# An interaction-layer kernel on one core: where a block's x is loaded, when two table copies are issued, and in which order TensorE prepares the weights

## The chip, the core and the metric

The kernel runs on one core of a Trainium2 chip. The metric is the device time of one execution in microseconds; it is 734.55 us before the change (median of 3 runs, 734.49 to 734.55). The engines are named as in the profile: PE is the matrix engine, PEld its weight loads, DVE the vector engine, ACT the scalar engine, POOL the general-purpose engine, SP the engine that only issues transfers. A "q" behind an engine's name is its sequencer, which issues transfers.

## The reference

For 1024 samples with F = 39 fields of E = 64 numbers, three layers each multiply every channel by every field and mix the products. The output is a weighted sum of the channels of all layers:

```
X0 = sparse_embedding                                    # (1024, 39, 64)
Xk = X0
for W, b in ((W0, b0), (W1, b1), (W2, b2)):              # 64 channels each
    Xk = einsum('bhe,bfe,ohf->boe', Xk, X0, W) + b
    outs.append(Xk.sum(axis=-1))
return concatenate(outs) @ fc_w.T + fc_b                 # (1024, 1)
```

Only sums over e and over the last layer's channels are needed, so the last two layers can be contracted with the weights before x is touched. With V2[h,f] = sum over o of fc_w2[o] W2[o,h,f], and T[k,g,f] = sum over h of V2[h,f] W1[h,k,g], the third layer's share is the sum over k of X1[k] times a quadratic form of x with the weights T[k]. The second layer's share is the sum over k of X1[k] times a linear form in x. The kernel therefore computes, for each column (one sample, one e), 128 quadratic forms of x: 64 with W0 and 64 with T. It multiplies the halves with each other and sums over e.

## The kernel before, in words

**Stream.** The 65,536 columns are cut into 32 blocks of 2048. A block's x lies in a DRAM table `xd` as 39 rows of 2048 numbers and a row of ones (40 rows for each block, two blocks in one table, three tables). POOL gathers rows of the table into five tiles of 128 partitions (`roll`, L176; an indirect transfer each, L172). Their row labels are such that products of two tiles (six pairs of tiles, `PAIRS`) hold nearly all products of two fields; the rest comes from two smaller tiles `u` and `v`, once for two blocks (`roll_small`, L181). DVE makes a product `p` of 128 x 2048 (L217), and PE multiplies it with a chunk of the weights `wa` in four quarters of 512 columns (L557), six chunks a block. Four products are in flight (`AHEAD`, the pool `prods`). When a block's six chunks and the small chunk (L577, L588) are done, ACT and DVE finish it (`finish`, L611). PE, DVE, ACT and POOL each run their instructions in the order written.

**Start.** The first block is special. Its x is loaded in two halves, each into a small table `xh` of its own (`load_half`, L248, on ACT's queue, among the loads of `w2s`, `w0s` and `w1s`). POOL gathers tiles 0 to 3 of it half by half from `xh` (L385: gathers 1 to 4 for the first half, 5 to 8 for the second). Between gathers 4 and 5 it issues `load(1, nc.gpsimd)` (L387), the load of the second block's x (1248 rows of 256 bytes, DRAM to DRAM, into `xd`). SP copies both halves from `xh` into the table `xd` as soon as they have landed (L389). Tile 4 of the first block is gathered from that table (`roll(0, (4,))`, L390), then `u` and `v`, which need both blocks' rows, and the five tiles of the second block (`roll(1)`, L470). Behind these POOL loads the biases, and writes the row of ones of the third table (`fill_ones(2, ...)`, L476).

**Weights.** Meanwhile PE and DVE prepare the weights, in this chain: `fc2` from `fc_w` (L353); PE contracts W2 with it into `pv` (L399); DVE transposes that into `blocks` (L420); PE spreads it over the partitions (`spread_v2`, L433); DVE multiplies it with a mask into `v2` (L448); PE multiplies W1 with `v2` (L480), which gives T; DVE transposes T in four pieces into `flat` (L489); ACT and DVE copy these into `both` (L496, L499). W0 goes through seven transposes on PE (`turn_w0`, L411) and four ACT copies into the other half of `both` (L459). Then `weight_rows` (L513) adds symmetric entries into `pairs`, a chunk at a time, `weight_turn` (L534) transposes a chunk on PE, and ACT copies it into `wa`. `spin` (L274) gives PE a matmul of constants whose result nobody reads; a dummy.

**First products.** For the first three chunks the products are made in pieces: two of 512 columns or one of 1024 in the first half, and the second half (1024 columns each, L687) only behind all of these. PE runs the first two quarters of the chunks 0, 1 and 2 (L692), then the other two of each. From chunk 3 on (`steps[3]`, L688) products are whole.

**Waiting.** Transfers issued by POOL count on eight semaphores in turn, so a ninth one waits until the first has landed. POOL's transfers share one queue (q0 in the profile), SP's are on q1, ACT's on q10.

The lines that set what waits for what in the first block's x:

```
for k, cols in enumerate(halves):
    for i in range(4):
        gather_rows(rt[0][:, i, cols], xh[k], i)
    if not k:
        load(1, nc.gpsimd)
for k in (1, 0):
    nc.sync.dma_start(xd[0][0:F, halves[k]], xh[k])
roll(0, (4,))
```

Of the kernel before, what the change touches and what calls it, by code (L numbers as in the profile page):

```python
# [54 lines left out]
F32 = mybir.dt.float32  # L55
I32 = mybir.dt.int32
AF = mybir.ActivationFunctionType
ALU = mybir.AluOpType
AX = mybir.AxisListType

B, F, E, H = 1024, 39, 64, 64
FH = F * H
FT = F + 1
# [3 lines left out]
NT = 5  # L67
# [8 lines left out]
MM = 512  # L76
# [69 lines left out]
def cin_kernel(ctx: ExitStack, tc: tile.TileContext, x, w0t, b0, w1, b1, w2, b2, fc_w, fc_b, out):  # L146
    nc = tc.nc
# [3 lines left out]
    const = ctx.enter_context(tc.tile_pool(name="const", bufs=1))  # L151
# [6 lines left out]
    xd = [dram.tile([2 * FT, BLK], F32, name=f"xd{k}") for k in range(NTAB)]  # L158
    xh = [dram.tile([F, SUB], F32, name=f"xh{k}") for k in range(2)]
# [4 lines left out]
    def load(n, engine=nc.sync):  # L164
        first = n % 2 * FT
        engine.dma_start(  # L166
            xd[n // 2 % NTAB][first : first + F].rearrange("f (b e) -> f b e", e=E),
            xv[:, n * BB : (n + 1) * BB, :],
        )

    def gather_rows(dst, table, k):
        nc.gpsimd.indirect_dma_start(  # L172
            dst, None, table, bass.IndirectOffsetOnAxis(ap=lists[:, k : k + 1], axis=0)
        )

    def roll(n, tiles=range(NT)):  # L176
        for i in tiles:
            k = n % 2 * NT + i
            gather_rows(rt[n % 2][:, i], xd[n // 2 % NTAB][: FT if k < NT else 2 * FT], k)

    def roll_small(n):  # L181
        table = xd[n // 2 % NTAB].rearrange("f (t c) -> (f t) c", c=SUB)
        for k, dst in enumerate((ut, vt)):
            gather_rows(dst[n // 2 % 2], table, 2 * NT + k)
# [6 lines left out]
    bias = const.tile([H, 2], F32, name="bias")  # L191
    b1s = const.tile([128, 1], F32, name="b1s")
    b0s = const.tile([128, 1], F32, name="b0s")
    fc0s = columns[:, 1:2]
    fcb = const.tile([1, 1], F32, name="fcb")
# [3 lines left out]
    lists = const.tile([128, 2 * NT + 2], I32, name="lists")  # L199
# [4 lines left out]
    ones = const.tile([16, 2, 128], F32, name="ones")  # L204
    ones1 = const.tile([16, 2, 128], F32, name="ones1")

    both = const.tile([128, F * FT], F32, name="both")
    pairs = const.tile([128, NCHUNK, 128], F32, name="pairs")
    unit = const.tile([128, 128], F32, name="unit")
# [13 lines left out]
    with prep as prep:  # L223
# [24 lines left out]
        def load_half(k):  # L248
            nc.scalar.dma_start(
                xh[k].rearrange("f (b e) -> b f e", e=E), x[k * SB : (k + 1) * SB]  # L250
            )
# [3 lines left out]
        nc.scalar.dma_start(w0s, w0t.rearrange("b (s a) h -> (b s) (a h)", s=NW))  # L255
        nc.scalar.dma_start(w1s, w1.rearrange("o (s n) -> (o s) n", s=2))
        load_half(1)
        nc.gpsimd.iota(place, pattern=[[0, 1]], base=0, channel_multiplier=1)
        nc.gpsimd.iota(apart, pattern=[[1, 128]], base=0, channel_multiplier=-1)
        nc.scalar.copy(warm, warm)  # L260
# [13 lines left out]
        def spin(n=1, cols=MM // 2):  # L274
            for _ in range(n):
                nc.tensor.matmul(  # L276
                    idle[:, 0:cols],
                    nc.const_aps.tensor(1.0, (128, 128), F32),
                    nc.const_aps.tensor(1.0, (128, cols), F32),
                    start=True,  # L280
                    stop=True,
                )
# [9 lines left out]
        def new():  # L292
            used[0] += 1
            return tmp[:, used[0] - 1 : used[0]]
# [7 lines left out]
        def fused(out, x, scalar, y, op0, op1):  # L302
            nc.vector.scalar_tensor_tensor(out, x, scalar, y, op0, op1)
# [15 lines left out]
        def turn(dst, row):  # L319
            nc.tensor.matmul(dst, row, one, start=True, stop=True)  # L320
# [4 lines left out]
        def turn_twice(at, row, k):  # L325
            turn(small[:, at : at + 1], row[:, k].rearrange("p h s -> p (h s)"))
# [7 lines left out]
        bothv = both.rearrange("p (a b) -> p a b", b=FT)  # L334
        nc.gpsimd.memset(bothv[0:H, :, F], 0.0)
        turn_twice(0, fcrow2, 1)
        spin()

        nc.vector.tensor_copy(row, place)
        step(row, F, 1.0, j)  # L340
# [20 lines left out]
        def fill_ones(k, engine, src):  # L361
            engine.dma_start(xd[k][F::FT].rearrange("r (p c) -> p r c", c=128), src)
# [10 lines left out]
        r, most, seat, far = (new() for _ in range(4))  # L373
        both_of = prep.tile([128, 2], F32, name="both_of")
        jumps = prep.tile([128, 2], F32, name="jumps")
# [6 lines left out]
        halves = [slice(0, SUB), slice(SUB, BLK)]  # L382
        for k, cols in enumerate(halves):
            for i in range(4):
                gather_rows(rt[0][:, i, cols], xh[k], i)  # L385
            if not k:
                load(1, nc.gpsimd)  # L387
        for k in (1, 0):
            nc.sync.dma_start(xd[0][0:F, halves[k]], xh[k])  # L389
        roll(0, (4,))  # L390

        blocks = prep.tile([128, 2, 320], F32, name="blocks")
        w2v = w2s.rearrange("p (h f) -> p h f", f=F)
        for k in range(2):
            for u in range(2):
# [6 lines left out]
                    stop=True,  # L404
                )

        turn_twice(6, fcrow2, 0)

        def turn_w0(k):
            n = min(128, NF * H - k * 128)  # L410
            nc.tensor.transpose(  # L411
                pw[k // 4][0:n, k % 4 * NW * F : (k % 4 + 1) * NW * F],
                w0s[:, k * 128 : k * 128 + n],
                unit[0 : NW * F, 0 : NW * F],
            )

        for k in range(3):
            turn_w0(k)
        for k in range(2):
            nc.vector.transpose(  # L420
                blocks[:, k].rearrange("p (f h) -> p f h", h=32),
# [4 lines left out]
        step(row, 64.0, 2.0 * FT - 1.0, far)  # L426
        nc.vector.tensor_reduce(jumps, steps_at, AX.X, ALU.add)
        fused(most, r, 4.0, most, ALU.add, ALU.add)
        column = blocks.rearrange("h k (f j) -> h (k f) j", j=32)[:, :, 0]

        def spread_v2(u, lo, n):
            rows = slice(H * u, H * u + H)
            nc.tensor.matmul(  # L433
                pv[u][:, 0:n],
                twice[rows].rearrange("p h s -> p (h s)"),
                column[rows, lo : lo + n],
                start=True,
                stop=True,
            )

        spread_v2(0, 0, 20)
        spread_v2(1, 1, 19)
        for k in range(3, 7):
            turn_w0(k)
        spin(1, MM // 4)
        nc.vector.tensor_scalar(v2v[:, 0, :, F - 32], mask, small[:, 6:7], None, ALU.mult)
        for u, at, low, lo, n in ((0, 0, 1, 0, 20), (1, 0, 1, 20, 12), (1, 12, 0, 0, 7)):
            nc.vector.tensor_tensor(  # L448
# [7 lines left out]
        for k, n in enumerate((8, 5)):  # L456
            for t in range(2):
                m = (n + 1 - t) // 2
                nc.scalar.copy(  # L459
                    both3[0:H, :, 8 * k + t : 8 * k + t + 2 * m - 1 : 2, 0:F],  # L460
                    pw[k][H * t : H * t + H, 0 : m * NW * F].rearrange(
                        "h (a b s) -> h s a b", b=F, s=NW
                    ),
                )
        nc.vector.tensor_tensor(seat, seat, far, ALU.add)
        nc.vector.tensor_tensor(both_of[:, 0:1], most, jumps[:, 0:1], ALU.add)
        nc.vector.tensor_tensor(both_of[:, 1:2], both_of[:, 0:1], jumps[:, 1:2], ALU.add)
        nc.vector.tensor_scalar(lists[:, 2 * NT :], both_of, 2.0, seat, ALU.mult, ALU.add)
        roll_small(0)
        roll(1)  # L470
        for h in (0, H):
            nc.gpsimd.dma_start(b0s[h : h + H], b0.rearrange("(h o) -> h o", o=1))
        for k, t in enumerate((b1, b2)):
            nc.gpsimd.dma_start(bias[:, k : k + 1], t.rearrange("(h o) -> h o", o=1))
        nc.gpsimd.dma_start(fcb, fc_b.rearrange("(p o) -> p o", o=1))
        fill_ones(2, nc.gpsimd, ones)  # L476
        w1v = w1s.rearrange("o (h f) -> o h f", f=F)
        groups = [(k, min(NA * k, F - NA)) for k in range(4)]
        for k, a in groups:
# [8 lines left out]
        for k, a in groups:  # L488
            nc.vector.transpose(  # L489
                flat[:, k], pt[k][:, 0 : 32 * NA].rearrange("p (h f) -> p f h", f=NA)  # L490
            )
        for k, a in groups:
            new = NA * k - a
            rows = slice(NA * k, a + NA)
            copy = nc.scalar.copy if k < 3 else nc.vector.tensor_copy
            copy(bothv[H:128, rows, 0:32], flat[H:128, k, new:])  # L496
            if k > 1:
                first = slice(0, 3) if k == 2 else slice(k, k + 1)
                nc.scalar.copy(  # L499
                    bothv[H:128, NA * first.start : rows.stop, 32:FT].rearrange(  # L500
                        "h (k a) b -> h k a b", k=first.stop - first.start
                    ),
                    flat[0:H, first, new:, 0 : FT - 32],
                )
# [164 lines left out]
    p = {}  # L669
# [18 lines left out]
    n, c = steps[3]  # L688
# [8 lines left out]
    for at, (n, c) in enumerate(steps[:-TAIL]):  # L697
# [33 lines left out]
        if at + AHEAD < len(steps):  # L731
            n, c = steps[at + AHEAD]
# [70 lines left out]
```

## Time and profile before

| | us |
|---|---|
| median of the runs (3) | 734.55 |
| the profiled execution's own time | 734.99 |
| its span, from first to last instruction | 733.2 |
| PE busy | 727.5 (99%) |
| DVE busy | 638.9 (87%) |
| POOL busy | 377.6 (51%) |
| ACT busy | 167.7 (23%) |
| mean transfer rate | 269 GB/s |
| one matmul record of L557, 128x512, two for each quarter | 0.594 (0.429 from start to start) |
| product on DVE, 128x2048 | 2.28 |
| product on DVE, 128x1024 | 1.22 |
| gather's issue on POOL, median | 0.94 |

Times inside the span are counted from its first instruction. [...] An idle time in brackets is that of the engine just before the instruction, with what ended it.

### The profile page before, as it was taken

The page shows a single profiled execution, that of the slowest core. Times are in us where ns is not written, and L with a number is a line of the kernel's source. Part 1 is how long each engine was busy: PE and PEld are TensorE (multiplying, and loading weights), DVE is VectorE, ACT ScalarE, POOL GpSimd, SP SyncE. Part 2 cuts the span into 40 slices and gives each one's busy share as a digit, 9 for nine tenths or more (in the row PEclk, how much of TensorE's full clock was granted, in tenths as well). Part 3 has the DMA queues.
Part 4 walks back from the last instruction along what each step waited for, and adds up shares of the span by engine and source line. Part 5 has one row for each costly group of instructions (what it writes and reads, how often), then busy time and mean ns, then how long its engine had stood idle before and what let it go on. Part 6 is the DMA issues. An engine that isn't in the chain of part 4 may idle for free.

```text
span 733.2 us, 6352 instructions
## 1 busy us (share of the span) xinstructions
PE 727.5 (99%) x2377; PEld 314.9 (43%) x2377; DVE 638.9 (87%) x520; ACT 167.7 (23%) x241; POOL 377.6 (51%) x254
## 2 busy tenths in 40 slices
PE   9999999999999999999999999999999999999998
PEld 4344444444444444444444444444444444444443
DVE  6998889988889888898988889888898888889885
ACT  3332121222212222121221212221122221212222
POOL 6858754537555455654547545455654447535300
PEclk9999999999999999999999999999999999999999
DMA  8999967779585796757778676886767876566700
GB/s 264 419 296 381 377 263 276 282 286 323 223 279 238 287 354 261 264 236 265 310 286 299 236 286 228 313 347 224 274 244 276 314 286 259 201 270 245 287 0 1
DMA packets 65979, 197.23 MB, mean 269 GB/s; under 512 B 40109, under 2 KB 40174, under 8 KB 45980
## 3 DMA queue, kind: packets, MB, share of 16 engines
q0 software_dynamic: 28784, 185.56, 65.5%
q1 hardware_dynamic: 35464, 9.28, 5.5%
q10 hardware_dynamic: 1700, 1.99, 0.9%
q8 instruction: 18, 0.29, 0.2%
q14 instruction: 13, 0.11, 0.0%
HBM read 196.76 MB, written 10.60 MB: 283 GB/s over the span
## 4 chain that ended last, share of the span: by engine, by line
PE 97%; DMA 1%; POOL 1%; DVE 1%; issue 0%; ACT 0%; DVEq 0%
PE po L557 90%; PE po L577 4%; PE po L588 2%; DMA r<-xh,lists 1%; POOL r L172 1%; PE idle L276 0%; PE pv L399 0%; DVE p L217 0%; POOL xd L166 0%; PE tr L541 0%; DVE g L607 0%; DVE sums L629 0%; ACT z L605 0%; PE small L320 0%; DVE blocks L420 0%
## 5 line engine op out<-in xcount | busy, mean ns | idle before, releaser
L557 PE MATMUL po<-p,wa 128*128 128x512 f32 x1536 | 665.9, 594 | 0.7 <-DVE p L217 0.5
L217 DVE TENSOR_TENSOR p<-r 128x2048 f32<-128x2048 f32 (+2 forms) x197 | 434.4, 2236 | 74.2 <-PE po L557 72.7
L557 PEld LDWEIGHTS po<-p,wa 128*128 128x128 f32 x1536 | 289.6, 190 | 371.5 <-issue 348.5
L172 POOL DMA_INDIRECT r<-xd,lists x156 | 299.6, 1920 | 289.9 <-issue 275.2
L605 ACT ACTIVATE z<-po,columns 64x512 f32<-64x512 f32 x128 | 87.4, 683 | 375.0 <-PE po L588 220.1
L607 DVE SCALAR_TENSOR_TENSOR g<-po,b0s,z 64x512 f32<-64x512 f32 x128 | 95.9, 749 | 9.3 <-ACT z L605 5.3
L600 ACT COPY g<-r 39x1024 f32<-39x1024 f32 x64 | 66.7, 1043 | 149.2 <-DVE sums L618 120.4
L618 DVE TENSOR_REDUCE sums<-g 103x16 f32<-103x1024 f32 x62 | 75.6, 1220 | 2.1
L172 POOL DMA_INDIRECT u<-xd,lists x16 | 30.3, 1891 | 5.0 <-issue 4.6
L172 POOL DMA_INDIRECT v<-xd,lists x16 | 29.7, 1854 | 4.9 <-issue 4.9
L577 PE MATMUL po<-p,wa 32*64 32x512 f32 x512 | 31.6, 600 | 0.0
L219 DVE TENSOR_TENSOR p<-u,v 128x1024 f32<-128x1024 f32 x16 | 19.5, 1217 | 0.0
L577 PEld LDWEIGHTS po<-p,wa 32*64 32x64 f32 x512 | 9.4, 131 | 20.2 <-issue 20.2
L588 PE MATMUL po<-u,wa 32*64 32x512 f32 x256 | 17.0, 587 | 0.0
L172 POOL DMA_INDIRECT r<-xh,lists x8 | 8.1, 1006 | 4.6 <-DVE blocks L420 2.5
L588 PEld LDWEIGHTS po<-u,wa 32*64 32x64 f32 x256 | 5.7, 132 | 8.0 <-issue 8.0
L276 PE MATMUL idle<-const-float32-1.0 128*128 128x512 f32 (+2 forms) x12 | 6.7, 649 | 0.8 <-PEq L790 0.8
L524 DVE TENSOR_TENSOR pairs<-both 128x2 f32<-128x2 f32 (+27 forms) x59 | 6.1, 171 | 0.1
L542 ACT COPY wa<-tr 128x128 f32<-128x128 f32 x8 | 2.1, 266 | 15.4 <-PE tr L541 15.4
L166 POOL DMA_DIRECT2D xd<-in_x x3 | 3.2, 1070 | 0.0
L276 PEld LDWEIGHTS idle<-const-float32-1.0 128*128 128x128 f32 x12 | 2.6, 257 | 1.0 <-issue 0.7
L541 PE MATMUL tr<-unit,pairs 128*128 128x128 f32 x8 | 2.3, 287 | 0.6 <-ACT wa L543 0.5
(96 smaller groups left out, 56.5 us busy)
## 6 DMA issues: line engine op xcount, KB each, us to landing
xd<-in_x SPq DMA_DIRECT2D x28, 312.0 KB
r<-xd,lists POOLq DMA_INDIRECT x156, 9.1
xd<-in_x POOLq DMA_DIRECT2D x3, 312.0 KB, 7.7
w2s<-in_w ACTq DMA_DIRECT2D x1, 624.0 KB
w1s<-in_w ACTq DMA_DIRECT2D x1, 624.0 KB
w0s<-in_w0t ACTq DMA_DIRECT2D x1, 380.2 KB
xh<-in_x ACTq DMA_DIRECT2D x2, 156.0 KB
xd<-xh SPq DMA_DIRECT2D x2, 156.0 KB
```

Of the source, the lines that this page charges most:

```text
L172: nc.gpsimd.indirect_dma_start(dst, None, table, bass.IndirectOffsetOnAxis(ap=lists[:, k : k + 1], axis=0))
L217: nc.vector.tensor_tensor(p[:, cols], r[:, i, cols], r[:, k, cols], ALU.mult)
L219: nc.vector.tensor_tensor(p[:, 0:SUB], ut[n // 2 % 2], vt[n // 2 % 2], ALU.mult)
L276: nc.tensor.matmul(idle[:, 0:cols], nc.const_aps.tensor(1.0, (128, 128), F32), nc.const_aps.tensor(1.0, (128, cols), F32), start=True, sto ...
L524: nc.vector.tensor_tensor(out, diagonal(a, b, sa, sb), diagonal(b, a, sb, sa), ALU.add)
L557: nc.tensor.matmul(po[n][m], wa[:, c, side : side + 2 * H], p[:, bass.ts(m, MM)], start=n % 2 == 0 and c == 0, stop=n % 2 == 1 and c == NP ...
L577: nc.tensor.matmul(dst[half * H : half * H + H], wa[rows, NPAIR, at : at + H], p[rows, bass.ts(side, MM)], start=t >= 2, stop=t < 2 and ha ...
L588: nc.tensor.matmul(dst[half : half + H], wa[rows, NPAIR + 1, H : 2 * H], ut[n // 2 % 2][rows, bass.ts(side, MM)], start=False, stop=t < 2,)
L600: nc.scalar.copy(gt[H : H + F], rt[n % 2][0:F, 0, bass.ts(m, SUB)])
L605: nc.scalar.activation(z[one], po[n][m][other], AF.Identity, bias=fc0s[other])
L607: return lambda: nc.vector.scalar_tensor_tensor(g[n][m // 2][0:H, at], po[n][m][one], b0s[one], z[one], ALU.add, ALU.mult)
L618: nc.vector.tensor_reduce(sums[:, b_at : b_at + SB], g[n][m // 2].rearrange("p (b e) -> p b e", e=E), AX.X, ALU.add,)
```

## The change

The load of the second block's x is issued by ACT, behind its five other loads, and no longer by POOL between gathers 4 and 5. SP's two copies of the first block's x into the table, the gather of tile 4, and all that POOL issues behind it are written after the four transposes into `flat`. Ahead of SP's copies stands a new transfer on SP, the row of ones of the third table, from a new tile `ones2` that DVE sets just after those transposes; it takes the place of the one that POOL issued at L476. SP issues in order, so the copies wait until T is transposed. On PE the dummy ahead of the contraction of W2 has 384 columns instead of 256; a dummy of 256 columns is new behind that contraction; V2's spreading comes ahead of all seven transposes of W0 (three stood before it); a dummy of 512 columns is new behind the spreading, and the one of 128 columns stands between the fourth and the fifth transpose of W0. One of the four copies of W0 goes from ACT to DVE. Four small DVE instructions that compute the lists of `u` and `v` move ahead of the masks of `v2`.

```
--- before.py
+++ after.py
@@ -204,6 +204,8 @@
+    ones2 = const.tile([64, 2, 32], F32, name="ones2")
@@ -255,6 +257,7 @@
         load_half(1)
+        load(1, nc.scalar)
@@ -334,7 +337,7 @@
         turn_twice(0, fcrow2, 1)
-        spin()
+        spin(1, 3 * MM // 4)
@@ -383,14 +386,6 @@
                 gather_rows(rt[0][:, i, cols], xh[k], i)
-            if not k:
-                load(1, nc.gpsimd)
-        for k in (1, 0):
-            nc.sync.dma_start(xd[0][0:F, halves[k]], xh[k])
-        roll(0, (4,))
@@ -404,6 +399,7 @@
+        spin()
         turn_twice(6, fcrow2, 0)
@@ -414,8 +410,6 @@
-        for k in range(3):
-            turn_w0(k)
@@ -426,6 +420,10 @@
         fused(most, r, 4.0, most, ALU.add, ALU.add)
+        nc.vector.tensor_tensor(seat, seat, far, ALU.add)
+        nc.vector.tensor_tensor(both_of[:, 0:1], most, jumps[:, 0:1], ALU.add)
+        nc.vector.tensor_tensor(both_of[:, 1:2], both_of[:, 0:1], jumps[:, 1:2], ALU.add)
+        nc.vector.tensor_scalar(lists[:, 2 * NT :], both_of, 2.0, seat, ALU.mult, ALU.add)
@@ -440,9 +438,12 @@
         spread_v2(1, 1, 19)
-        for k in range(3, 7):
+        spin(1, MM)
+        for k in range(4):
             turn_w0(k)
         spin(1, MM // 4)
+        for k in range(4, 7):
+            turn_w0(k)
@@ -456,24 +457,13 @@
-                nc.scalar.copy(
+                copy = nc.vector.tensor_copy if (k, t) == (0, 1) else nc.scalar.copy
+                copy(
...
-        (the four list instructions, roll_small(0), roll(1), the loads of the biases)
-        fill_ones(2, nc.gpsimd, ones)
@@ -489,6 +479,20 @@
                 flat[:, k], pt[k][:, 0 : 32 * NA].rearrange("p (h f) -> p f h", f=NA)
             )
+        nc.vector.memset(ones2, 1.0)
+        nc.sync.dma_start(
+            xd[2][F::FT].rearrange("r (p c) -> p r c", c=32), ones2
+        )
+        for k in (1, 0):
+            nc.sync.dma_start(xd[0][0:F, halves[k]], xh[k])
+        roll(0, (4,))
+        roll_small(0)
+        roll(1)
+        for h in (0, H):
+            nc.gpsimd.dma_start(b0s[h : h + H], b0.rearrange("(h o) -> h o", o=1))
+        for k, t in enumerate((b1, b2)):
+            nc.gpsimd.dma_start(bias[:, k : k + 1], t.rearrange("(h o) -> h o", o=1))
+        nc.gpsimd.dma_start(fcb, fc_b.rearrange("(p o) -> p o", o=1))
```

More of the change, by code (lines that the diff above doesn't have):

```diff
@@ L464, in cin_kernel @@
                 )
[L465 to L475, printed above, removed]
-        fill_ones(2, nc.gpsimd, ones)
         w1v = w1s.rearrange("o (h f) -> o h f", f=F)
```

## The prediction

> **What bounds the kernel now.** I read the page's busy times first (PE 99%), then the chain of waits in order of time, then the timeline of the first 50 us, then the transfers by stretches. From 24 us on the chain is PE alone, but for an ACT copy at 38 us (0.47 us), up to a tail of 2.8 us. What the change can move is the moment at which PE's unbroken row begins. The chain ahead of it:
>
> ```profile
> 11.80 1.07 POOL xd L166
> 12.87 0.30 issue
> 13.18 0.98 POOL r L172
> 14.16 0.31 issue
> 14.47 8.09 DMA r<-xh,lists
> 22.56 0.03 issue
> 22.61 0.04 issue
> 22.65 1.24 DVE p L217
> 23.89 0.14 issue
> 24.02 4.53 PE po L557 x10
> ...
> 28.66 0.86 PE po L557 x2
> 29.52 0.13 issue
> 29.65 1.10 PE po L557 x2
> ```
>
> Columns: start, length, what. Gather 6 is issued at 14.47 and lands at 22.56; the product behind it ends at 23.89, and PE goes on at 24.02. At 29.52 PE waits once more, for chunk 3's product. The timeline tells who is late by how much (in brackets the idle time before, and what ended it):
>
> ```profile
> 9.55 0.36 DVE L448 TENSOR_TENSOR v<-pv,mask 128x40 f32<-128x40 f32 x3 [1.22 <-PE pv L433]
> 9.77 1.66 SPq L389 DMA_DIRECT2D xd<-xh  x2
> 10.73 2.34 PE L480 MATMUL pt<-w1s,v 128*128 128x320 f32 x4
> 12.86 1.42 PE L480 MATMUL pv<-w1s,v 128*128 128x320 f32 x4
> 18.58 1.66 POOL L172 DMA_INDIRECT r<-xd,lists  x1 [0.31 <-issue]
> 20.25 1.21 DVE L217 TENSOR_TENSOR p<-r 128x1024 f32<-128x1024 f32 x1
> 22.65 3.68 DVE L217 TENSOR_TENSOR p<-r 128x1024 f32<-128x1024 f32 x3 [1.20 <-DMA r<-xh,lists]
> 27.58 2.88 POOL L172 DMA_INDIRECT r<-xd,lists  x1 [0.31 <-issue]
> ```
>
> DVE is through with the first halves at 21.46 and idle for 1.20. So the whole weight preparation (W2 to V2 to T to `pairs`) has 1.20 us of slack: the gathers, not it, set the start. The next two products start at 23.89 and 25.11, each the moment gather 7 or 8 has landed (the trace has 23.86 and 25.08). From 25.11 DVE is unbroken: the third product, eleven entries of `pairs`, chunk 3's product, done at 29.50. So PE's row from 29.65 hangs on gather 8.
>
> The last view is busy time by stretches; the last three columns are granted clock, busy share of the transfer engines, and GB/s:
>
> ```profile
> 12.00:14.00 2.00, 2.00 (x7) 1.31 (x6) 1.30 (x3) 0.80 (x2) 1.70 (x2) 1.00 0.94 225
> 14.00:16.00 2.00, 2.00 (x11) 0.81 (x10) 1.80 (x8) 1.37 (x5) 1.39 (x3) 1.00 0.94 320
> 18.00:22.00 4.00, 3.73 (x10) 1.33 (x9) 3.46 (x14) 1.55 (x5) 3.27 (x3) 1.00 1.02 407
> ```
>
> Gathers land, by the trace, at 12.06, 13.53, 16.97, 18.36, (the load 19.52), 21.28, 22.56, 23.86, 25.08. In the undisturbed stretch one takes 1.28 (22.56 less 21.28). Gather 3 takes 3.44 after gather 2, just when SP's copies run: their packets are seen from 13.5 to 17. That is 2.16 too much for copies of 0.32 MB.
>
> **The change, part by part.** The sum goes against the profiled execution (734.99, span 733.2, 1.79 outside it); the runs' median is 0.44 lower, and I take the difference off the median.
>
> Load of the second block's x. POOL no longer spends 1.07 and 0.30 ahead of gather 5. But gather 6 waited 8.09 in the queue, so earlier issue alone brings nothing; what counts is the 1.16 that the load took of the queue (18.36 to 19.52). [...] Bounds for gather 8: gain 1.16 (all lies in gaps; at 12 to 14 us only 225 GB/s moved) to loss 0.24 (1248 packets of 18 ns on 16 engines, 1.40, instead of 1.16). I take a gain of 0.2, since SP's later loads, packets of the same kind, went beside gathers at about one for one (45 to 57 a us, 28 to 40 us): some 70 to 80% of it then still runs ahead of gather 8. ACT's own price: the issue (SP's first loads: 0.88 and, behind a full queue, 8.92) delays its table load and the zeroing of `pairs`, which end at 6.12 with nothing due before 9.94; 3.8 us of cover, gone only if the issue hangs.
>
> [...]
>
> SP's copies. They go from 9.77 to behind T, 14.83 and a transfer of about 0.34 (SP's earlier row of ones): 15.2. Before, first packets came about 4 us behind the issue; so 19 to 22, on top of gathers 6 to 8. Gathers 3 to 5 win 2.16. Gather 8 wins between 0 (all copies still ahead of it) and 2.16 (all behind it); I take 0.9, a little under the middle, as 19 to 22 lies before 25. With the 0.2: gather 8 at 24.0 instead of 25.08. Gather 6 falls to 20.5 or so, before DVE can use it (21.46).
>
> What is queued behind the copies: tile 4, `u`, `v`, the second block's five tiles and the biases, all on POOL. The copies land some 5.7 us behind their last issue (11.44 to 17.15 before), so at 22.5, and tile 4 is issued then, not at 18.58. Its landing was 27.58, 9.0 behind its issue with a full queue; gather 1, into a free queue, took 5.05 (half the size), the first of block 2 8.35 (45.15 to 53.50). POOL may be held too: the gather issued at 27.58, beside DVE's product, took 2.88 instead of 0.94 and ended 0.95 behind that product. So tile 4 lands between 27.5 and 34 (held by products until 25.2, then 8.4); I take 29, nearest to the free queue. Chunk 4's product (2.28) was done at 32.42, PE came to it at 34.40. With PE 1.1 earlier the tile is due at 31.0. Cost zero, at the upper end 3. The second block's tiles have 5 to 6 us (tile 1 landed at 35.37; PE needs its product at 44.02).
>
> V2 and the dummies. Between W2's contraction and the spreading stood three transposes of W0 (8.14 to 8.90). Now a dummy of 256 columns stands there (such a pair took 1.22 at 3.37): the spreading comes at 8.6, gain 0.3. Between spreading and T: before, 9.45 to 10.73. Now a dummy of 512 (2.05 at 0.78 us, 1.02 at 14.11), seven transposes (0.2 each at 8.14; about half that at full rate) and one of 128: 3.8 at the slow rate, 2.2 at the fast. T's matmuls show both rates: 2.34 for four, then 1.42; the granted clock stands at 1.00 in all windows, but the throttle's first record in the trace begins at 13.05. If full rate comes there again, T ends 0.95 later; if one turn earlier, all of T is fast and it ends about 0.5 earlier. With 0.09 for the memset of `ones2` on DVE: +1.0 to -0.4 on DVE's readiness. I take -0.2. Against 1.20 of slack this costs nothing at either end while gathers bind, but at +1.0 DVE would be ready at 22.5 and its three products end 0.15 earlier than before only. The copy of W0 on DVE (0.54 on ACT) lies in DVE's idle 1.49 before T; the four list instructions (0.6) in its 1.22 before V2's masks.
>
> [...]
>
> Sum: 0.2 + 0.9 on gather 8; DVE reaches the third product at max(24.0, 21.3 + 2.45 = 23.75), so 24.0; PE's row at 28.55 instead of 29.65. Gain 1.1: 734.55 - 1.1 = 733.45, I say 733.5.
>
> **The rivals.** First, copies wholly behind gather 8, the load in gaps and a faster T: gather 8 at 21.8, DVE at 20.8 + 2.45 = 23.3; gain 1.8, 732.7. For it: 225 GB/s at 12 to 14 us. Against it: PE's and DVE's own work between 15.4 and 21.5 is unbroken.
>
> Second, nothing: the engines have the same bytes to move before gather 8, or full clock again at 13.05 eats the 1.20 of slack. 734.3 to 734.7.
>
> Third, the other side: tile 4 is late. It decides if it lands after 31.0, each us then costs one. At 34 it is 3.0 less the 1.1 won: 736.4. For it: POOL held behind products (2.88, 2.60 and, at 50.98, 5.75), in order before seven more gathers. Against it: before, three issues at 22.58 to 25.07 slipped in at 0.94 each beside the half products.
>
> **How the numbers follow.** Chances: gain 0.5 to 1.45 as summed, 0.44; first rival 0.28; nothing 0.13; late tile 0.15. A difference under 0.2% (1.47 us) can't be told from none here. Faster by more (under 733.08): the first rival's and a little of the sum's, 0.3. Slower by more (over 736.02): half of the late tile and a mishap in issue, 0.12; with what else the new order of POOL may hold, 0.17. Within: 0.53. The range keeps 0.8 by reaching from 732.2 (0.5 below the first rival) to 736.0; the sum's own is 733.1 to 734.1.
>
> **What would show it.** Right: gather 8 landing at 23.5 to 24.5, the half products starting at 21.3 without the 1.20 of idle time, chunk 3's first matmul at 28.6, and no idle PE after it. The clock shows in T's eight matmuls: all at 1.42 for four. Wrong: PE idle at 32 to 35 us behind tile 4; T's matmuls ending past 15; ACT's zeroing of `pairs` past 9; SP's copies still seen beside gathers 6 to 8 with these at their old times.

## The result, and the profile after

The changed kernel takes 738.67 us (median of 9 runs, 736.03 to 740.62) against 734.23 us (733.84 to 734.90) before: 1.0057 times as long, 95% interval 1.0045 to 1.0069. It is slower by 4.4 us where I had forecast 733.5, and 2.7 above the upper end of the range, 736.0. The profiled execution takes 739.11 (span 737.3) against 734.99 (733.2).

The chain of waits, columns as before:

```profile
14.89 0.26 ACT pairs L526
15.15 4.34 another core or an unknown queue
19.50 0.26 ACT wa L546
19.75 0.04 issue
19.80 2.07 PE po L561 x2
21.87 0.21 PE tr L545
22.08 3.41 PE po L561 x4
25.50 0.21 PE tr L545
25.71 6.96 PE po L561 x16
```

Gathers are gone from the chain. In their place stand 4.34 us that end in ACT's copy of the first transposed chunk into `wa` (L546), and the view can't say what ended them: there is only one core. The copy waits for one thing, the transpose on PE (TensorE is another name for PE). The timeline of the same stretch tells when that was done; the second fence is the same step before:

```profile
15.99 0.30 PE L545 MATMUL tr<-unit,pairs 128*128 128x128 f32 x1
16.12 0.60 PE L279 MATMUL idle<-const-float32-1.0 128*128 128x256 f32 x2
17.13 1.90 DVE L219 TENSOR_TENSOR p<-r 128x512 f32<-128x512 f32 x3
19.48 0.27 ACT L546 COPY wa<-tr 128x128 f32<-128x128 f32 x1 [4.32 <-remote]
19.80 2.07 PE L561 MATMUL po<-p,wa 128*128 128x512 f32 x2 [3.07 <-ACT wa L546]
19.84 4.63 DVE L219 TENSOR_TENSOR p<-r 128x1024 f32<-128x1024 f32 x4
22.80 2.63 POOL L172 DMA_INDIRECT r<-xd,lists  x1 [5.55 <-DMA xd<-xh]
25.38 2.28 DVE L219 TENSOR_TENSOR p<-r 128x2048 f32<-128x2048 f32 x1
```

```profile
16.36 0.30 PE L541 MATMUL tr<-unit,pairs 128*128 128x128 f32 x1
16.70 0.27 ACT L542 COPY wa<-tr 128x128 f32<-128x128 f32 x1 [1.02 <-PE tr L541]
17.02 1.12 PE L557 MATMUL po<-p,wa 128*128 128x512 f32 x2
27.23 2.27 DVE L217 TENSOR_TENSOR p<-r 128x2048 f32<-128x2048 f32 x1
```

The transpose ends at 16.29; ACT starts at 19.48. Before, the same step took 0.04 us (16.66 to 16.70), so TensorE's signal is 3.15 late. The trace's records of the semaphores say the same: TensorE's four signals of that time, one from a matmul that ended at 14.87, the dummy's, the transpose's and the next dummy's, are recorded at 19.378, 19.421, 19.455 and 19.497. They come 34 to 43 ns apart, though the work that they tell of ended over 1.9 us (14.87 to 16.72): by the trace the work was done 2.8 to 4.5 us before its signals are recorded. I call this **late signals**. Between 8 and 20 us the trace also has only 72 records of signals, against 205 before; 54 and 163 of these tell of transfers that landed.

The DVE lines show that the part I had forecast worked: four half products without the 1.20 of idle time, chunk 3's product at 25.38 and not at 27.23. Nobody could use it, because PE stood still for 3.07 us.

What that did to the clock (last three columns: granted clock, share of the transfer engines, GB/s):

```profile
16.00:20.00 4.00, 0.93 (x4) 0.53 (x5) 4.00 (x23) 0.51 (x4) 1.06 (x1) 0.87 1.02 392
20.00:24.00 4.00, 4.00 (x6) 1.75 (x7) 4.00 (x4) 0.45 (x3) 1.20 (x1) 0.50 0.46 185
24.00:28.00 4.00, 4.00 (x9) 1.72 (x8) 4.00 (x17) 2.23 (x4) 3.70 (x2) 0.78 0.47 162
```

PE has work from 19.80 on, and runs at half rate until 25.77. The account: the first product of chunk 0 starts at 19.80, not 17.02 (+2.78). From there to the end of the first block's matmuls it takes 28.03 us, not 27.07 (+0.96): half rate for 5.97 us loses 2.98, and without it the same work would take 25.05, since PE finds its products ready. So the first block ends at 47.83, not 44.09 (+3.74). From there to the last matmul both take 686.77. The tail is 0.36 longer. Together 4.1, the difference of the spans.

Last, the page's transfer queues, of the changed kernel and (second fence) of the kernel before:

```profile
q0 software_dynamic: 28640, 185.22, 64.5%
q10 hardware_dynamic: 2961, 2.31, 1.1%
```

```profile
q0 software_dynamic: 28784, 185.56, 65.5%
q10 hardware_dynamic: 1700, 1.99, 0.9%
```

ACT's queue has 1,261 packets more. In the trace 1,248 of these are of 256 bytes (the other 13 of 4); POOL's queue had moved the same 0.32 MB in 78 packets of 4,096 bytes. Between 7 and 12 us the trace has 2,213 packets, not 985. Such packets are not new in themselves: before, too, ACT's queue moved 1,248 of 256 bytes (the first block's halves, 3.66 to 9.36 us), and no signal was late.

### The profile page after: what moved, and what is told of

Same layout as the page of the kernel before. It is cut to its first block, busy times and chain, and to the rows that moved or that the text cites. A ratio compares the mean times of both kernels' runs of the same rounds, so it can differ in the third digit from the quotient of the medians.

```text
span 737.3 us, 6362 instructions
## 1 busy us (share of the span) xinstructions
PE 729.5 (99%) x2381; PEld 315.4 (43%) x2381; DVE 639.5 (87%) x522; ACT 166.9 (23%) x240; POOL 380.2 (52%) x252
## 4 chain that ended last, share of the span: by engine, by line
PE 97%; ACT 1%; another core or an unknown queue 1%; issue 0%; DVE 0%; POOL 0%; ACTq 0%
PE po L561 90%; PE po L581 4%; PE po L592 2%; PE idle L279 0%; PE pv L394 0%; ACT both L500 0%; ACT both L461 0%; PE tr L545 0%; PE small L323 0%; DVE g L611 0%; DVE sums L633 0%; ACT z L609 0%; ACT both L503 0%; ACT wa L546 0%
## 5 line engine op out<-in xcount | busy, mean ns | idle before, releaser
L172 POOL DMA_INDIRECT u<-xd,lists x16 | 32.1, 2006 | 4.9 <-issue 4.6
L279 PE MATMUL idle<-const-float32-1.0 128*128 128x512 f32 (+3 forms) x16 | 9.2, 665 | 0.8 <-PEq L794 0.8
L546 ACT COPY wa<-tr 128x128 f32<-128x128 f32 x8 | 2.1, 266 | 20.5 <-PE tr L545 16.2
```

The costliest lines, as they stand in the source:

```text
L172: nc.gpsimd.indirect_dma_start(dst, None, table, bass.IndirectOffsetOnAxis(ap=lists[:, k : k + 1], axis=0))
L279: nc.tensor.matmul(idle[:, 0:cols], nc.const_aps.tensor(1.0, (128, 128), F32), nc.const_aps.tensor(1.0, (128, cols), F32), start=True, sto ...
```

## The experiments

The runs were made in five groups, each on one chip (by the recorded numbers chip 1 for groups 1, 3 and 5, chip 15 for group 2, chip 11 for group 4), with runs of the kernel before among them. "Late" is the time from the end of the first transpose to ACT's copy, "records" the trace's records of signals between 8 and 20 us, both of the profiled execution; the kernel before has only one profile.

| kernel | group | median us | ratio to before, interval | late us | records |
|---|---|---|---|---|---|
| before | | 734.2 to 734.7 | | 0.04 | 205 |
| changed | | 738.67 | 1.0057 [1.0045, 1.0069] | 3.19 | 72 |
| a_load_on_act | 1 | 733.16 | 0.9985 [0.9967, 1.0003] | 0.04 | 234 |
| b_copies_behind_T | 1 | 737.11 | 1.0031 [1.0017, 1.0044] | 0.04 | 187 |
| c_order_only | 1 | 735.21 | 1.0003 [0.9993, 1.0014] | 0.04 | 209 |
| d_load_back | 1 | 736.40 | 1.0031 [1.0007, 1.0055] | 0.04 | 184 |
| e_copies_back | 2 | 738.54 | 1.0050 [1.0027, 1.0072] | 2.65 | 69 |
| h_tile4_halves | 2 | 740.59 | 1.0081 [1.0064, 1.0097] | 3.95 | 64 |
| after_again | 2 | 737.64 (one) | | 3.19 | 74 |
| after_third | 2 | 735.44 (one) | | 3.21 | 84 |
| e_no_dummies | 3 | 733.85 | 0.9985 [0.9975, 0.9994] | 0.04 | 212 |
| a_dummies | 3 | 733.36 | 0.9988 [0.9976, 1.0000] | 0.04 | 212 |
| e_load_sp | 3 | 739.39 | 1.0056 [1.0040, 1.0071] | 0.04 | 202 |
| a_again | 3 | 734.32 | 0.9996 [0.9987, 1.0005] | 0.04 | 223 |
| after_no_dummies | 4 | 737.41 | 1.0040 [1.0025, 1.0054] | 1.00 | 99 |
| after_no_512 | 4 | 738.45 | 1.0050 [1.0033, 1.0067] | 1.84 | 89 |
| h_no_dummies | 4 | 739.72 | 1.0073 [1.0056, 1.0090] | 3.06 | 50 |
| a_double | 4 | 739.40 | 1.0073 [1.0044, 1.0102] | 4.76 | 52 |
| after_beside | 5 | 738.62 | 1.0058 [1.0041, 1.0074] | 1.09 | 83 |
| a_beside | 5 | 739.92 | 1.0066 [1.0046, 1.0086] | 4.09 | 63 |

### Each part alone (group 1)

Only the load on ACT (a, an edit of the kernel before):

```diff
         load_half(1)
+        load(1, nc.scalar)
...
-            if not k:
-                load(1, nc.gpsimd)
```

> Only the load of the second block's x moves to ACT's queue; SP's copies, the dummies and the order of PE's work stay as before. In the changed kernel's trace TensorE's first transpose of the weights ends at 16.29 us but its signal reaches ACT only at 19.46, with TensorE's three signals around it (19.38 to 19.50), and PE is idle for 3.07 us. Theory 'load': this packet burst (867 packets in the microsecond from 9 us) behind five other loads on ACT's queue brings on the late signal: 736 to 740 us, PE idle 2 to 5 us ahead of the first matmuls of L557. Theory 'copies' (SP's 128-byte rows of ones and the copies beside it do it): no late signal, POOL's 1.37 us back, 733.5 to 734.3. Theory 'order' (earlier full clock and V2 ahead of W0's transposes do it): the same 733.5 to 734.3.

733.16, no late signals. The same step as above, from its timeline:

```profile
14.33 0.30 PE L540 MATMUL tr<-unit,pairs 128*128 128x128 f32 x1
14.67 0.27 ACT L541 COPY wa<-tr 128x128 f32<-128x128 f32 x1 [1.02 <-PE tr L540]
14.98 1.13 PE L556 MATMUL po<-p,wa 128*128 128x512 f32 x2
```

Gather 8 lands at 22.86, 2.2 earlier than before, and the first block's matmuls end at 41.88, 2.2 earlier. Theory "load", which asked for 736 to 740, looked dead. It was not, as group 5 shows.

Only SP's copies, with the row of ones ahead of them and all that POOL issues behind (b; the loads of the biases move with them):

```diff
-        for k in (1, 0):
-            nc.sync.dma_start(xd[0][0:F, halves[k]], xh[k])
-        roll(0, (4,))
...
-        roll_small(0)
-        roll(1)
...
-        fill_ones(2, nc.gpsimd, ones)
...
                 flat[:, k], pt[k][:, 0 : 32 * NA].rearrange("p (h f) -> p f h", f=NA)
             )
+        nc.vector.memset(ones2, 1.0)
+        nc.sync.dma_start(
+            xd[2][F::FT].rearrange("r (p c) -> p r c", c=32), ones2
+        )
+        for k in (1, 0):
+            nc.sync.dma_start(xd[0][0:F, halves[k]], xh[k])
+        roll(0, (4,))
+        roll_small(0)
+        roll(1)
...
```

> Only SP's copies, behind a new transfer of ones in 128-byte rows, go behind T, with all that POOL issues behind them; the load stays on POOL between gathers 4 and 5 and PE's order is that of before. Theory 'copies': 736 to 740, PE idle 2 to 5 us ahead of the first matmuls of L557 with its signals late. Theories 'load' and 'order': no late signal, gather 8 lands 0.5 to 1.5 us earlier than 25.08, 733.0 to 734.2.

737.11: a loss of its own, and not by late signals. Its chain of waits:

```profile
15.52 0.87 SPq L488
...
16.51 7.48 DMA xd<-xh
...
24.72 7.89 DMA r<-xd,lists
...
32.73 2.30 DVE p L219
35.03 0.14 issue
35.17 1.10 PE po L562 x2
```

The copies land at 23.99, 7.48 after the start of their last issue; tile 4 is issued at 24.72 and lands at 32.61; PE waits 1.78 for its product. And gather 8 gains nothing: the copies now run beside gathers 6 to 8, which land at 21.60, 23.80 and 25.02 (25.08 before). The first block's matmuls end at 46.06, 1.97 later than before, the 1.78 and a little.

Only the order (c): the dummies, V2 ahead of W0's transposes, one copy on DVE and the four list instructions, as in the front part's diff, with load and copies as before.

> Only the dummies, V2's spreading ahead of W0's transposes, the one W0 copy on DVE and the place of the four list instructions; load and copies as before. Theory 'order': 736 to 740 with PE idle 2 to 5 us ahead of the first matmuls of L557. Theories 'load' and 'copies': DVE ready 0.4 us earlier but still waiting for gather 6 at 22.56, 734.0 to 734.6, no difference that can be measured.

735.21, no difference that can be told (0.9993 to 1.0014). The clock went to full only at 12.94 there, and T came late:

```profile
13.06 1.33 PE L480 MATMUL pt<-w1s,v 128*128 128x320 f32 x4
14.24 1.32 PE L480 MATMUL pv<-w1s,v 128*128 128x320 f32 x4
```

Before, these stood at 10.73 and 12.86. The first transpose of the weights ends 1.38 later (18.04), and the slack ahead of gather 6 covers it but for 0.34 at the end of the first block.

The changed kernel with the load back on POOL (d):

```diff
-        load(1, nc.scalar)
...
+            if not k:
+                load(1, nc.gpsimd)
```

> The changed kernel with the load of the second block's x back on POOL between gathers 4 and 5, all else as changed. Theory 'load': the late signal is gone, 732.8 to 734.2. Theories 'copies' and 'order': it stays, 736 to 740. If only both a and d are slow, the parts work together.

736.40, no late signals, and yet not the 732.8 to 734.2 that theory "load" gave: behind T the copies stay. In its profile tile 4 is issued at 25.50, after copies that land at 24.78; the first block's matmuls end at 44.98, 0.89 later than before, and PE waits 1.01 at 58.9 for a tile of the next pair of blocks. Single runs go up to 741.46; what these hold was not seen.

### Copies back, tile 4 without them, and the changed kernel again (group 2)

The changed kernel with copies, tile 4 and what follows in their old place (e):

```diff
+        for k in (1, 0):
+            nc.sync.dma_start(xd[0][0:F, halves[k]], xh[k])
+        roll(0, (4,))
...
+        roll_small(0)
+        roll(1)
...
+        fill_ones(2, nc.gpsimd, ones)
...
-        nc.vector.memset(ones2, 1.0)
-        nc.sync.dma_start(
-            xd[2][F::FT].rearrange("r (p c) -> p r c", c=32), ones2
-        )
-        for k in (1, 0):
-            nc.sync.dma_start(xd[0][0:F, halves[k]], xh[k])
-        roll(0, (4,))
-        roll_small(0)
-        roll(1)
...
```

> The changed kernel with SP's copies, tile 4's gather and all that POOL issues behind it back in their old place (copies when the halves have landed, the third table's ones on POOL from the old tile); the load stays on ACT's queue and PE's order stays as changed. Theory 'late tile 4' (the copies land at 22 to 25 us, tile 4 is issued only then and lands at 30 to 33, PE waits for its product): the loss is gone, 732.0 to 734.0, tile 4 landed by 28 us. If load and PE's order together hold up TensorE's signals: 736 to 740 still, with PE idle for 2 to 5 us ahead of the first matmuls of L557.

The copies kept behind T, but tile 4 gathered from the small tables (h):

```diff
-    xh = [dram.tile([F, SUB], F32, name=f"xh{k}") for k in range(2)]
+    xh = [dram.tile([FT, SUB], F32, name=f"xh{k}") for k in range(2)]
+        for k in range(2):
+            nc.sync.dma_start(
+                xh[k][F:FT].rearrange("r (p c) -> p r c", c=128), ones[0:8, 0:1]
+            )
...
+        for k, cols in enumerate(halves):
+            gather_rows(rt[0][:, NT - 1, cols], xh[k], NT - 1)
...
-        roll(0, (4,))
```

> The changed kernel, the copies still behind T, but tile 4 no longer waits for them: it is gathered in two halves from the same small tables as tiles 0 to 3 (which get a row of ones each from SP at the start), as ninth and tenth gather. Theory 'late tile 4': tile 4's second half lands at 24 to 27 us, no PE idle at 32 to 36, 732.0 to 734.5 (0.3 to 1 more than with the copies back, since u, v and the second block's tiles are still issued behind the copies). Theory 'late u, v and second block' or 'late signals': 735.5 to 740.

> The changed kernel unchanged, to see which wait is there in another execution. Theory 'late tile 4': clock full at 12 to 13 us, T at 15 to 16, copies landed at 24 to 25, tile 4 landed at 31 to 33, PE idle 1 to 3 us ahead of the chunk that needs it (as 1.78 with the copies alone). Theory 'late signals': TensorE's signal around the first transpose of the weights late by 2 to 4 us again.

> The same once more: the two theories as for the run before it.

"Late tile 4" fell as the whole explanation: with the copies back it still took 738.54, with tile 4 free of them 740.59. All four profiles have late signals (2.65 to 3.95). The two repeats show what else decides the time of one execution. Stretches of the second and of the third (granted clock is the third column from the end):

```profile
20.00:24.00 4.00, 4.00 (x8) 1.63 (x9) 4.00 (x4) 0.43 (x3) 1.22 (x1) 0.68 0.38 154
```

```profile
20.00:24.00 4.00, 4.00 (x12) 1.88 (x11) 3.86 (x5) 2.19 (x6) 1.45 (x2) 1.00 0.32 131
```

In the third, PE's first product of chunk 0 starts 0.73 earlier than in the first:

```profile
19.07 1.13 PE L561 MATMUL po<-p,wa 128*128 128x512 f32 x2 [3.09 <-ACT wa L546]
```

Signals are late by 3.2 in all three executions of the changed kernel seen so far, PE idle for 3.07 to 3.09. But half rate lasted two windows of 3.41 us in the first, one in the second, none in the third; the first block's matmuls end at 47.83, 46.25 and 44.16, the times are 739.11, 737.64 and 735.44. Half of the half-rate time plus the later start accounts for it: 44.16 + 0.73 + 2.98 = 47.87, and 44.16 + 0.70 + 1.41 = 46.27. So in these three the late signals use up what the gathers gained (44.16 against 44.09 before), and the clock makes most of the loss. It does not make it in every execution: of the nine behind the result four have a mean granted clock of 1.000, as the third here, and took 736.03, 736.87, 738.54 and 739.02. What else these hold was not seen; group 5 has a profile of one such execution.

### The dummies, and the load's time (group 3)

```diff
-        spin(1, 3 * MM // 4)
+        spin()
...
-        spin()
...
-        spin(1, MM)
```

taken from e (e_no_dummies), and the reverse put into a (a_dummies); and e with the load issued by SP behind its copies (e_load_sp), and a once more:

> The kernel with the copies back (load on ACT, PE's order as changed), but without the two new dummies of 256 and 512 columns and with the first back at 256: V2's spreading ahead of all W0 transposes stays. In all three executions of the changed kernel and in those with the copies back and with tile 4 from halves, TensorE's four signals around the first transpose come together 2.5 to 3.8 us late; with the load on ACT alone they do not. Theory 'dummies' (TensorE's extra work while the load's packets run brings it on): no late signals, 732.0 to 734.0. Theory 'order of V2' or 'load on ACT with anything that delays T': late signals, PE idle 2.5 us or more ahead of the first matmuls of L557, 735 to 742.

> The kernel with only the load on ACT (733.16), plus the three dummy changes at the same places but with W0's transposes in their old order. Theory 'dummies': TensorE's signals late by 2.5 us or more, 735.5 to 742. Theory 'order of V2': no late signals, 732.5 to 734.5.

> The kernel with the copies back and PE's order as changed, the load of the second block's x issued by SP behind its two copies (about 11.7 us) and no longer by ACT: the burst of 850 to 940 packets in the microsecond from 9 us is gone, the same bytes run at 14 to 20 us. Theory 'burst' (the load's packets at 8 to 11 us, whatever PE does, fill the path of signals): no late signals, 733.5 to 735.5 (gather 8 at 24 to 25.5 since the load now runs beside gathers 3 to 7). Theory 'dummies': the same, since with the load on POOL they did nothing either; if the signals are late here too, the load's time is not the cause.

> The load on ACT alone once more, as the candidate that beats both kernels: 732.1 to 733.6 in most executions, with the ratio's interval below 1; two of its eight executions took 735.6 and 735.9, and if those had late signals, the load alone brings them on now and then, and the median lies between 732.5 and 735.

No profile of this group has late signals. I read it as "it takes the dummies and the order together", which was wrong: the whole group had none. a_again missed what I had expected of it (732.1 to 733.6, the interval below 1): 734.32, no difference. Theory "burst" is not borne out here: a_dummies, a_again and e_no_dummies have the load on ACT, and their signals come in time (0.04); a path of signals that packets fill no run shows. e_load_sp, expected at 733.5 to 735.5, is slow for another reason; its load lands only 16.2 us after its issue, all POOL work behind it is late, and PE waits for the second block's tile, which brings half rate (45.56 to 52.39):

```profile
44.28 4.73 DVE L217 TENSOR_TENSOR p<-r 128x2048 f32<-128x2048 f32 x2 [6.87 <-DMA r<-xd,lists]
46.63 3.78 PE L556 MATMUL po<-p,wa 128*128 128x512 f32 x4 [3.14 <-DVE p L217]
```

### Parts of the changed kernel, and twice the load (group 4)

The dummies taken out of the changed kernel (as above), the one of 512 columns alone, the dummies out of h; and into a, the load a second time:

```diff
         load(1, nc.scalar)
+        nc.scalar.dma_start(
+            spare[0:F].rearrange("f (b e) -> f b e", e=E), xv[:, BB : 2 * BB, :]
+        )
```

> The changed kernel with the two new dummies taken out and the first back at 256 columns; load on ACT, copies behind T, V2 ahead of W0's transposes stay. With the copies back, taking the dummies out removed the late signals (738.54 to 733.85). Theory 'late signals are the loss': no late signals, 733 to 735; tile 4 may then wait for the copies. Theory 'late tile 4 is a loss of its own': PE idle 1 to 2.5 us ahead of the chunk that needs tile 4, 734.5 to 737. Theory 'the copies' place adds to the late signals': late signals still, 736 to 740.

> The changed kernel without the new dummy of 512 columns between V2's spreading and W0's transposes; the other two dummy changes stay. If this dummy is what it takes: no late signals, 733 to 735.5, about as without all three. If the dummy of 256 columns or the first, longer one is: late signals, 736 to 740.

> Tile 4 gathered in halves from the small tables, copies behind T, load on ACT, no new dummies. Theory 'late signals were the loss of that kernel too' (740.59 with dummies): no late signals, no wait for tile 4, gathers 3 to 8 not disturbed by copies: 732.0 to 734.0, the best of all if u, v and the second block's tiles come in time; 734.5 to 737 if these are late (PE idle at 40 to 60 us).

> The load on ACT alone, PE's order and dummies as before, and the same load once more behind it into a spare table that nobody reads: twice the packets of 256 bytes at 8 to 13 us. Theory 'dose' (enough packets at that time hold up TensorE's signals whatever its order): signals late by 2 us or more, 736 to 741. Theory 'it takes the dummies': no late signals; gathers 1 to 8 land 0.5 to 1.5 us later for the added bytes, 733.5 to 735.5.

Late signals in all four, so neither the dummies nor V2's order is needed: a_double has the order of before and the longest delay. Its T was done at 13.99 and DVE heard of it at 17.46; then

```profile
19.53 0.43 PE L544 MATMUL tr<-unit,pairs 128*128 128x128 f32 x1 [3.31 <-issue]
24.73 0.27 ACT L545 COPY wa<-tr 128x128 f32<-128x128 f32 x1 [5.88 <-remote]
25.04 2.07 PE L560 MATMUL po<-p,wa 128*128 128x512 f32 x2 [4.22 <-ACT wa L545]
```

3.31 and 4.22 us of idle PE, 7.5 together. The loss of after_no_dummies, 2.8 us, is only in part one of signals: in its profile PE is idle for 0.89 behind them, for 1.48 (until 34.02) behind a product that waited for tile 4, and for 0.65 (until 59.49).

### Side by side (group 5)

> The changed kernel unchanged, on the same chip as the run beside it. The runs so far stood on three chips: on chip 1 no profile had late signals, with or without the load on ACT; on chips 11 and 15 every profile had them, and every kernel there had the load on ACT. So what was put down to dummies may be the chip. Theory 'chip': on chip 1 no late signals here, records of signals complete, 734.5 to 737.5 with PE idle 1 to 2.5 us for tile 4; on another chip late signals by 2.5 us or more and 736 to 740. Theory 'dummies and order': late signals on any chip.

> The load on ACT alone, on the same chip as the changed kernel beside it. Theory 'chip': on a chip where the changed kernel has late signals, this one has them too, PE idle 2 us or more ahead of the first matmuls of L556 and 735 to 740; on chip 1 neither has them and this takes 732.5 to 734.5. Theory 'dummies and order': none here in either case, 732.5 to 734.5, while the changed kernel has them.

a_beside is a, unchanged, on the same chip number as in groups 1 and 3. Its chain:

```profile
12.83 0.26 ACT pairs L521
13.09 5.06 another core or an unknown queue
18.15 0.02 issue
18.17 0.27 ACT wa L541
18.45 0.04 issue
18.49 2.07 PE po L556 x2
```

4.09 late, 3.97 of idle PE, half rate until 24.16; 739.92 us is the median, the profiled execution took 737.48. So in this group the load on ACT alone brings the whole loss (5.4 us), with the old order, the old dummies and the copies in their old place; theory "dummies and order" is refuted, and "chip" too as far as the number names one chip, since it is that of the runs without. All six executions of a here have a mean granted clock of 0.993 to 0.998, all nineteen of groups 1 and 3 one of 0.999 or 1.000: it is the group that differs, not a single execution. The changed kernel beside it had a smaller delay (1.09) and full clock throughout; there tile 4 shows, and PE waits once more until 60.25 (0.84):

```profile
32.16 2.29 DVE L219 TENSOR_TENSOR p<-r 128x2048 f32<-128x2048 f32 x1 [2.02 <-DMA r<-xd,lists]
34.59 1.10 PE L561 MATMUL po<-p,wa 128*128 128x512 f32 x2 [0.69 <-DVE p L219]
```

**What is shown.** Late signals and missing records come together in 11 profiles (late by 1.0 to 4.8, 50 to 99 records) and both are absent in the 9 others (0.04; 184 to 234). All 11 have the load on ACT. The five kernels without it, which have 913 to 994 packets between 7 and 12 us and not some 2,200, show none in a profile; but four of these profiles come from groups 1 and 3, where the kernels with the load on ACT have none either. What tells is the time: the kernel before took 734.45, 734.59 and 734.55 in the very groups in which the kernels with the load on ACT lost 2.8 to 6.1 us (after_third's single run 1.0), and in group 5 a, which differs from it by the load alone, lost 5.4. A second loss, copies behind T, comes without late signals: 2.5 us alone (b).

**What stays open.** Four profiles with the load on ACT (groups 1 and 3) have no late signals. What differs from group to group is not in the kernels. Packets on ACT's queue are what the load adds. That their number does it fits a_double's two delays (7.5 us, 4.0 with a single load), but these stand in two groups, a_double was not run where there are no late signals, and b, c, d and e_load_sp not where there are: that the other parts of the change could not do the same there is not shown. Why the signals come late I can't show. Late signals and missing records go together in the 20 profiles, but no run shows that one brings the other, and none here was made without recording, so whether recording has a part in it stays untested. The changed kernel itself was not profiled without late signals; what it would take then is not known, and d (736.40) is the nearest run.

No version beats the kernel before for sure: the load on ACT alone gave 0.9985, 0.9996 and 1.0066 in three groups. e_no_dummies (0.9975 to 0.9994) has the same load on ACT and was run in group 3 only.

## Why the prediction was wrong, point by point

**The load's gain: mis-sized.** I took 0.2 on gather 8 within -0.24 to +1.16. Where signals were not late it was 2.2 (22.86 in a), beyond the upper end. I had let the packets run at the gathers' pace, with a part left behind gather 8; that was my estimate from SP's later loads, and no run shows such a pace for the load on ACT's queue. In a the last of them starts at 10.83, ahead of gather 2's landing (13.71): 837 packets of ACT's queue start in the microsecond from 9, where SP's later loads had some 45. Between 7 and 12 us the transfer engines moved 331 GB/s in a, against 277 before.

**ACT's price: the step that failed.** "3.8 us of cover, gone only if the issue hangs": the issue took 1.05, and `pairs` was zeroed by 7.23, inside the cover as forecast. I had priced a transfer by its issue and its share of the transfer engines, and put everything else at nothing. That signals of PE come 3 us late with the load on ACT's queue was in none of my rivals, and no row of before showed it: there, late was 0.04. In the changed kernel it cost 3.15 at ACT and 3.07 of idle PE; in group 5, with nothing else changed, 3.97.

**The copies' gain: mis-sized.** 0.9 for gather 8; alone (b) it was 0.06, near the lower end, 0: the copies ran at 18 to 23 us, beside gathers 6 to 8.

**Gather 8 at 24.0: right in direction, too small.** In the changed kernel its last recorded part lands at 23.12, outside the 23.5 to 24.5 that I had named, and chunk 3's product starts 1.85 earlier. The gain is 1.96 and not 1.1; both terms were wrong, one too small and one too large, and that their errors partly cancel is luck.

**V2 and the dummies: too narrow.** -0.2 within -0.4 and +1.0. With full clock at 8.70 T's matmuls were all fast and its last transpose ended 0.58 earlier (14.25); with full clock at 12.94 (c) the weights came 1.38 later. The moment at which full clock comes varies from profile to profile: 6.67 to 14.48 here. Both ends lie outside my range. In time it cost nothing that can be told (c: 735.21), as argued. The "turn" by which I let full clock come earlier is 3.41 us in the changed kernel's trace, where the clock stands at full for 10.24 us and at half for 6.83, three and two times that; full clock came 4.35 earlier, not one turn.

**Late tile 4: the rival was real, but not what made the loss in the profiled execution.** In the changed kernel it landed at 29.96 (forecast 29) and was not waited for, PE being late itself. Alone (b) it landed at 32.61, late by 1.6 against the 31.0 I gave, and cost 1.78 of the 3 I had set as upper end.

**Another issuer.** It saved more than issue time: gather 8 came 2.2 us earlier in a, where POOL's issue and the pause behind it took 1.07 and 0.30. And on ACT's queue the same bytes went in packets of 256 bytes, not 4,096 as on POOL's. Which engine moved a packet the traces here don't tell.

**The forecast's clock.** I had the clock only as something to gain earlier. That a stall on PE's row is paid again in half rate (2.98 here) was missing from every rival's price.

## What to carry to other kernels

When a transfer changes its issuing engine, compare the packets that each queue makes of it (1,248 of 256 bytes on ACT's here, 78 of 4,096 on POOL's), not only the bytes, and look for late signals: a wait that the chain puts down to an unknown releaser (4.34 us here), while the work waited for has long ended (3.19 us before). Price a stall of the matrix engine with the half rate that may follow (here 5.97 us of it behind 3.07 of idle time), not with its own length alone. And run the same kernel in several groups before a part of it is blamed: the runs of groups 1 to 3 pointed at the dummies and the order, and kernel a, run again unchanged in group 5, refuted it.

## What the hardware showed that I had not expected

Signals of PE came 1.0 to 4.8 us behind finished work in 11 of 20 profiles; in the profile behind the result four of them are recorded 34 to 43 ns apart.

In these traces the granted clock falls for windows of 3.41 us (two in the changed kernel, 18.94 to 25.77, and one in its second execution), and a stall's place in the window decided. PE idle for 2.2 us of a window (the changed kernel: 16.72 to 18.94) or 2.5 (its second execution) brought half rate from the window's end; 1.5 and 1.6 us of idle time, a 3.09 us stall cut by a window's border (its third), brought none. All 20 traces fit: from full rate, windows with up to 1.78 us of idle PE (b) kept it, those with 2.06 or more (e_copies_back) lost it. After such a window, work for 2.55 of 3.41 us did not bring full rate back, 2.83 did.

Copies of 0.32 MB took 7.5 us from the start of their last issue when they ran beside gathers 6 to 8 (b), 6.45 before (10.70 to 17.15). In both places the gathers beside them were held up: gather 3 landed 3.44 behind gather 2 before, gathers 6 and 7 1.99 and 2.20 behind the ones ahead of them in b, where 1.28 was the undisturbed step.
